# A graph network's recurrent state loaded with two tiles interleaved instead of four, wider lags in the plan, and the TensorE transpose path for two tail groups instead of four

## The chip, the cores and the metric

One NeuronCore of a Trainium2 chip. The metric is the device time of one execution in microseconds (us), medians over several runs. All runs below are in the fast state (single core; granted TensorE clock 0.99 or more as the mean of nearly every run, named where not).

## The reference

`x` is 64 batches of 256 nodes with 128 features, `adj` is 256 x 256. Four layers follow each other, each with a residual and a layer norm. The last is a gated unit of five steps; that is where this change acts:

```python
def step(h, _):
    m_in = jnp.einsum('nm,bmd->bnd', in_matrix, h)     # both matrices are adj here
    m_out = jnp.einsum('nm,bmd->bnd', out_matrix, h)
    av = jnp.concatenate([m_in, m_out], axis=-1)
    u3 = h @ u3_w.T + u3_b
    z = jax.nn.sigmoid(av @ w3_w.T + w3_b + u3)
    r = jax.nn.sigmoid(av @ w4_w.T + w4_b + u3)
    hv = jnp.tanh(av @ w5_w.T + w5_b + (r * h @ u5_w.T + u5_b))
    h = (1.0 - z) * h + z * hv
    return (h, None)
```

## The kernel before

A group is two batches, so four tiles of 128 nodes x 128 features (512 floats in each of 128 partitions); there are 32 groups. Every instruction is entered into a plan with its engine, a cost and a lag (how long after its end another engine may use its result). The plan is made once, while the kernel is built; it fixes each engine's order. The hardware only follows that order and waits where data are not there yet.

```python
class Plan:
    def order(self):
        ...  # each time: of all engines' ready ops take the one that can start first;
                    key = (max(at, t0), op.rank, op.seq)     # then the lower group, then age
        ...
            op.start, op.end = start, start + op.cost + op.lag
            free[op.engine] = start + op.cost
```

The state hT has features in partitions, but the next propagate (`adj @ h`) needs nodes in partitions. Most groups turn it round without TensorE: VectorE transposes 32 x 32 blocks, one DMA writes the result to HBM, one loads it back. The last TAIL groups transpose on TensorE.

```python
def by_node(v):                                   # four tiles interleaved
    return v.ap.rearrange("p (n q) -> p q n", q=Q)

def propagate(self, tag, h, aTs, ins=None, outs=None):
    ps = self.val("bank", "pm" + tag)
    def run():
        o, a = (outs or plain)(ps), (ins or nat)(h)
        for b in range(NB):
            for kt in range(T):
                mm(o[b], a[:, b * T + kt, :], aTs[kt], kt == 0, kt == T - 1)   # h is the stationary operand
    self.pe(pe_cost(N, NB * T), run, [h], [ps])
    return self.copied("m" + tag, ps)

def packed(self, name, src):
    far = self.turned(name, src, "p (k q i) -> p q k i", "p (k j q) -> p q k j")
    t = self.val("w", name)
    def run():
        nc.sync.dma_start(t.ap.rearrange("p (r n) -> p r n", r=4),
                          far.ap.rearrange("(r i) (k n) -> (i k) r n", r=4, k=4))
    self.add("SP", 420, 2350, run, [far], [t])
    return t

# in each of five steps
    if g < G - TAIL:
        if s < STEPS - 1:
            h, ats, ins = self.packed(f"h{s}", hT), a1p, by_node
    else:
        pT = self.transposes(f"h{s}", hT)
        if s < STEPS - 1:
            h = self.copied(f"h{s}", pT)
```

## Time and profile before

| | before |
|---|---|
| time, median of first three runs | 1457.39 us |
| profiled span | 1455.1 us |
| TensorE busy | 97% |
| weight loads of h after DMA / natural | 326 / 190 ns |
| distance of propagate matmuls, h after DMA / natural | 233 / 216 ns |
| TensorE's gaps, 30 us to 185 us before the end | 22.8 us |
| TensorE's gaps in the last 185 us (the drain) | 17.1 us |

A **gap** in this document is worked out from the trace: the distance between the starts of two successive matmuls minus the median distance of matmuls of that kind, where that excess is over 25 ns. It counts all lost time before a matmul, whatever the cause. It is wider than the profile's view of waits, which counts only what exceeds the modelled end of the matmul before. Busy share cannot show it: TensorE reads 97% in both kernels.

### The profile page before, as it was taken

The numbers are of one execution on the slowest core, as the hardware profiler recorded it, in microseconds if no ns is written. First come the engines' busy times: TensorE is split into PE (matmuls) and PEld (weight loads), VectorE is DVE, ScalarE is ACT, GpSimd is POOL, SyncE is SP. The second block draws the span as 40 slices with busy tenths as digits, with TensorE's granted clock in tenths as the row PEclk, the third lists the DMA queues.
The fourth block names the chain that finished last, engine by engine and source line by source line (L and its number), as shares of the span: only waits on it lengthen the run. The fifth ranks groups of instructions, "written<-read, shape, count | busy, mean of one in ns | idle before, by whom it ended". The sixth has DMA issues, their size and how long they took to land.

```text
span 1455.1 us, 16313 instructions
## 1 busy us (share of the span) xinstructions
PE 1407.4 (97%) x5054; PEld 965.1 (66%) x5054; DVE 1008.5 (69%) x2696; ACT 515.7 (35%) x820; POOL 230.7 (16%) x199
## 2 busy tenths in 40 slices
PE   5999999999999999999999999999999999999995
PEld 4866676567666777667676667676677676656652
DVE  3756686758777686676876677776767768757734
ACT  1143423333333333333333333334333333344342
POOL 0411031101210122001211022111111112001200
PEclk9999999999999999999999999999999999999998
DMA  5022232323233223233222333223333322210000
GB/s 165 15 81 79 92 111 87 113 68 109 77 111 109 94 96 107 73 123 95 95 82 90 104 105 96 82 94 95 111 103 96 97 79 88 74 42 30 1 8 15
DMA packets 173830, 123.44 MB, mean 85 GB/s; under 512 B 12592, under 2 KB 148144, under 8 KB 173744
## 3 DMA queue, kind: packets, MB, share of 16 engines
q1 hardware_dynamic: 171440, 121.16, 26.2%
q10 hardware_dynamic: 2304, 1.25, 0.3%
q8 instruction: 40, 0.66, 0.2%
q14 instruction: 46, 0.38, 0.1%
HBM read 61.80 MB, written 60.29 MB: 84 GB/s over the span
## 4 chain that ended last, share of the span: by engine, by line
PE 47%; DVE 5%; DMA 1%; ACT 1%; issue 0%; POOL 0%; SPq 0%; POOLq 0%; DVEq 0%; ACTq 0%
PE pr L191 15%; PE pmg L191 10%; PE ph L191 10%; PE py L191 7%; PE pm L191 3%; PE pmq L191 1%; DVE y L382 1%; DMA h<-dh 1%; DVE d L455 1%; DVE e L455 1%; PE pth L406 1%; DVE st L357 1%; DVE hT L455 1%; ACT hv L449 0%; DVE s L373 0%
## 5 line engine op out<-in xcount | busy, mean ns | idle before, releaser
L368 POOL TENSOR_TENSOR rs<-ve,half 128x4 f32<-128x4 f32 x128 | 141.3, 1106 | 1120.3 <-DVE ve L362 1112.5
L191 PEld LDWEIGHTS pmg<-aTp,h 128*128 128x128 f32 x896 | 220.5, 326 | 39.0 <-DMA h<-dh 12.6
L191 PE MATMUL pmg<-aTp,h 128*128 128x256 f32 x896 | 231.1, 402 | 6.0 <-DMA h<-dh 5.6
L455 DVE TENSOR_TENSOR d<-hv,hT 128x512 f32<-128x512 f32 x160 | 114.3, 715 | 170.6 <-ACT hv L449 170.4
L455 DVE TENSOR_TENSOR rh<-r,hT 128x512 f32<-128x512 f32 x160 | 112.3, 702 | 143.2 <-ACT r L449 143.0
L349 ACT COPY mg<-pmg 128x512 f32<-128x512 f32 x160 | 93.7, 585 | 280.0 <-PE pmg L191 264.8
L382 DVE TENSOR_SCALAR y<-s,mv,rs 128x128 f32<-128x128 f32 x512 | 146.0, 350 | 56.5 <-POOL rs L368 56.0
L191 PE MATMUL pr<-hT,u3T 128*128 128x512 f32 x320 | 163.5, 596 | 3.5 <-DVE hT L455 3.1
L191 PE MATMUL pr<-mg,w4T 128*128 128x512 f32 x320 | 164.4, 595 | 2.3 <-ACT mg L349 2.3
L191 PE MATMUL pr<-mg,w34T 128*128 128x512 f32 x320 | 163.0, 594 | 0.1
L191 PE MATMUL ph<-mg,w5T 128*128 128x512 f32 x320 | 162.8, 592 | 0.0
L191 PE MATMUL ph<-rh,u5T 128*128 128x512 f32 x320 | 162.5, 593 | 0.0
L449 ACT ACTIVATE r<-pr,rb 128x512 f32<-128x512 f32 x160 | 110.0, 687 | 137.5 <-PE pr L191 129.0
L449 ACT ACTIVATE z<-pr,zb 128x512 f32<-128x512 f32 x160 | 109.9, 687 | 133.3 <-PE pr L191 128.4
L449 ACT ACTIVATE hv<-ph,hb 128x512 f32<-128x512 f32 x160 | 109.9, 687 | 48.3 <-PE ph L191 46.4
L414 DVE STREAM_TRANSPOSE th<-hT 128x512 f32<-128x512 f32 x112 | 124.4, 1111 | 1.4
L455 DVE TENSOR_TENSOR e<-z,d 128x512 f32<-128x512 f32 x160 | 115.6, 723 | 3.8
L455 DVE TENSOR_TENSOR hT<-hT,e 128x512 f32<-128x512 f32 x160 | 109.6, 686 | 2.5
L357 DVE BATCH_NORM_STATS2 st<-s 128x6 f32<-128x128 f32 x512 | 109.4, 278 | 1.2
L191 PEld LDWEIGHTS ph<-rh,u5T 128*128 128x128 f32 x320 | 60.4, 190 | 72.6 <-issue 56.9
L191 PEld LDWEIGHTS ph<-mg,w5T 128*128 128x128 f32 x320 | 60.8, 190 | 70.3 <-issue 56.7
L191 PEld LDWEIGHTS pr<-mg,w4T 128*128 128x128 f32 x320 | 59.0, 191 | 51.2 <-issue 43.8
(95 smaller groups left out, 1609.5 us busy)
## 6 DMA issues: line engine op xcount, KB each, us to landing
dh<-th SPq DMA_DIRECT2D x140, 256.0 KB, 2.0
h<-dh SPq DMA_DIRECT2D x112, 256.0 KB, 2.8
x<-in_x_dram SPq DMA_DIRECT2D x32, 256.0 KB, 3.4
out_dram<-y SPq DMA_DIRECT2D x32, 256.0 KB, 2.3
dx<-tx SPq DMA_DIRECT2D x30, 256.0 KB, 2.1
xT<-dx SPq DMA_DIRECT2D x120, 64.0 KB, 2.0
hT<-dh SPq DMA_DIRECT2D x112, 64.0 KB, 2.0
dn<-tn SPq DMA_DIRECT2D x28, 256.0 KB, 2.0
```

What stands on the lines that cost most here:

```text
L191: nc.tensor.matmul(o, lhsT, rhs, start=start, stop=stop, skip_group_check=shared)
L349: self.act(lambda: nc.scalar.copy(t.ap, ps.ap), [ps], [t])
L357: nc.vector.bn_stats(st.ap[:, q * 6:(q + 1) * 6], nat(s)[:, q, :])
L368: lambda: nc.gpsimd.tensor_tensor(rs.ap, ve.ap, half, op=OP.pow), [ve], [rs])
L382: nc.vector.tensor_scalar(nat(y)[:, q, :], nat(s)[:, q, :], mv.ap[:, 2 * q:2 * q + 1], rs.ap[:, q:q + 1], op0=OP.subtract, op1=OP.mult)
L406: nc.tensor.transpose(ps.ap[:, q * P:(q + 1) * P], src.ap[:, q * P:(q + 1) * P], ident)
L414: self.dve(dve_cost(512), lambda: nc.vector.transpose(t.ap.rearrange(outs, k=4, q=Q), src.ap.rearrange(ins, k=4, q=Q)), [src], [t])
L449: self.act(lambda: nc.scalar.activation(t.ap, ps.ap, func, bias=bias, scale=1.0), [ps], [t], act_cost(512) + 100)
L455: self.dve(dve_cost(512), lambda: nc.vector.tensor_tensor(t.ap, a.ap, b.ap, op=op), [a, b], [t])
```

## The change

Intent: make h's weight loads cheap by interleaving only the two tiles of one batch; pay with two DMAs. Let the plan count results and transfers as later than before, so that the fixed order waits less. Keep the TensorE transpose path for two groups.

```diff
-TAIL = 4
+TAIL = 2
@@ Plan.add
+        if engine == "SP":
+            lag += 700
@@
+    def tile_of(v, q):
+        return nat(v)[:, q, :]
+    def pair_of(v, q):
+        return v.ap.rearrange("p (b c t) -> p b t c", b=NB, t=T)[:, q // T, q % T, :]
@@ lags of results: PE, VectorE, ScalarE
-            return self.add("PE", cost, 200, run, reads, writes)
+            return self.add("PE", cost, 260, run, reads, writes)
-            return self.add("DVE", cost, 130, run, reads, writes)
+            return self.add("DVE", cost, 260, run, reads, writes)
-            return self.add("ACT", cost, 70, run, reads, writes)
+            return self.add("ACT", cost, 130, run, reads, writes)
@@ propagate
-                o, a = (outs or plain)(ps), (ins or nat)(h)
+                o, a = (outs or plain)(ps), ins or tile_of
                 ...
-                        mm(o[b], a[:, b * T + kt, :], aTs[kt], kt == 0, kt == T - 1)
+                        mm(o[b], a(h, b * T + kt), aTs[kt], kt == 0, kt == T - 1)
@@ packed
-            far = self.turned(name, src, "p (k q i) -> p q k i", "p (k j q) -> p q k j")
-            t = self.val("w", name)
+            turn, far, t = ...
+            self.dve(dve_cost(512), lambda: nc.vector.transpose(
+                turn.ap.rearrange("p (u j t) -> p u t j", t=T, j=32),
+                src.ap.rearrange("p (u t i) -> p u t i", t=T, i=32)), [src], [turn])
+            self.add("SP", 420, 2000, lambda: nc.sync.dma_start(far.ap, turn.ap), [turn], [far])
             def run():
-                nc.sync.dma_start(t.ap.rearrange("p (r n) -> p r n", r=4),
-                                  far.ap.rearrange("(r i) (k n) -> (i k) r n", r=4, k=4))
-            self.add("SP", 420, 2350, run, [far], [t])
+                for b in range(NB):
+                    nc.sync.dma_start(t.ap.rearrange("p (b r n) -> b p r n", b=NB, r=4)[b],
+                                      far.ap.rearrange("(r i) (k b n) -> b (i k) r n", r=4, b=NB, k=4)[b])
+            self.add("SP", 900, 2300, run, [far], [t])
@@ step
-                        h, ats, ins = self.packed(f"h{s}", hT), a1p, by_node
+                        h, ats, ins = self.packed(f"h{s}", hT), a1p, pair_of
```

More of the change, by code (lines that the diff above doesn't have):

```diff
@@ L431, in packed @@
         def packed(self, name, src):
-            far = self.turned(name, src, "p (k q i) -> p q k i", "p (k j q) -> p q k j")
-            t = self.val("w", name)
+            turn, far, t = self.val("w", "t" + name), self.val("dram", "d" + name), self.val("w", name)
+            self.dve(dve_cost(512), lambda: nc.vector.transpose(
+                turn.ap.rearrange("p (u j t) -> p u t j", t=T, j=32),
+                src.ap.rearrange("p (u t i) -> p u t i", t=T, i=32)), [src], [turn])
+            self.add("SP", 420, 2000, lambda: nc.sync.dma_start(far.ap, turn.ap), [turn], [far])
             def run():
-                nc.sync.dma_start(t.ap.rearrange("p (r n) -> p r n", r=4),
-                                  far.ap.rearrange("(r i) (k n) -> (i k) r n", r=4, k=4))
-            self.add("SP", 420, 2350, run, [far], [t])
+                for b in range(NB):
+                    nc.sync.dma_start(t.ap.rearrange("p (b r n) -> b p r n", b=NB, r=4)[b],
+                                      far.ap.rearrange("(r i) (k b n) -> b (i k) r n", r=4, b=NB, k=4)[b])
+            self.add("SP", 900, 2300, run, [far], [t])
             return t
```

## The prediction

> **What bounds the kernel now.** I read the page first: busy shares, then the 40 slices.
>
> ```profile
> PE 1407.4 (97%) x5054; PEld 965.1 (66%) x5054; DVE 1008.5 (69%) x2696; ACT 515.7 (35%) x820; POOL 230.7 (16%) x199
> PE   5999999999999999999999999999999999999995
> DMA  5022232323233223233222333223333322210000
> ```
>
> TensorE is busy from the second slice to the last but one; nothing else is over 69%. So time changes only where a matmul becomes quicker, where matmuls disappear, or where a gap before a matmul closes. Busy time alone does not say how much a matmul costs, so I next read the timeline of TensorE in mid-kernel. Columns: start, time to the end of the last instruction of the run, instruction, count.
>
> ```profile
> 702.29 2.03 PE L191 MATMUL pmg<-aTp,h 128*128 128x256 f32 x8
> 704.15 0.63 PE L191 MATMUL py<-w0s,xT 128*128 128x256 f32 x2
> ...
> 710.24 1.89 PE L191 MATMUL pm<-aT,y 128*128 128x256 f32 x8
> 711.97 2.03 PE L191 MATMUL pmg<-aTp,h 128*128 128x256 f32 x8
> 713.83 1.02 PE L191 MATMUL pr<-hT,u3T 128*128 128x512 f32 x2
> 714.69 1.05 PE L191 MATMUL py<-w1s,m 128*128 128x128 f32 x8
> ```
>
> Matmuls overlap, so the cost of a run is the distance from its start to the next start. Eight matmuls of 256 columns on natural data (pm) cost 711.97 - 710.24 = 1.73 us, 216 ns each. The same eight on the h that came back by DMA cost 704.15 - 702.29 = 1.86 and 713.83 - 711.97 = 1.86, 233 ns each. Why shows in the groups by form (busy, mean ns; then idle time before):
>
> ```profile
> L191 PEld LDWEIGHTS pmg<-aTp,h 128*128 128x128 f32 x896 | 220.5, 326 | 39.0 <-DMA h<-dh 12.6 <-PE pr L191 5.0 <-issue 4.7
> L191 PEld LDWEIGHTS pmg<-aT,h 128*128 128x128 f32 x128 | 23.8, 190 | 9.2 <-issue 3.6 <-ACT h L349 3.0
> L414 DVE STREAM_TRANSPOSE th<-hT 128x512 f32<-128x512 f32 x112 | 124.4, 1111 | 1.4
> L414 DVE STREAM_TRANSPOSE th<-y 128x512 f32<-128x512 f32 x28 | 19.7, 704 | 0.2
> ```
>
> h is the stationary operand. Where its four tiles are interleaved (one element in 16 bytes) a weight load takes 326 ns, natural 190 ns, and the slower load sets the pace of these short matmuls. The transpose that writes this layout takes 1111 ns against 704 ns for one with contiguous rows.
>
> Last I separated the gaps by time, taking each start-to-start distance minus the median of its kind. From 30 to 1270 us they add up to about 23 us, 13.6 of them before a pmg on a loaded h; from 1270 us to the last matmul about 17. TensorE's first group work starts at 23.8 us and the last matmul at 1446.7, so the head is 23.8 and the end after it 8.4 us. The waits and the transfers that the gaps point to:
>
> ```profile
> PEld pmg L191 <- DMA h<-dh: 12.6, 19, 1.6
> PE pmg L191 <- DMA h<-dh: 5.6, 11, 1.6
> PE pth L406 <- DVE hT L455: 10.1, 6, 3.0
> h<-dh SPq DMA_DIRECT2D x112, 256.0 KB, 2.8
> ```
>
> The third line lies wholly in the drain at the end (the same view over 1270 to 1456 us has the same 10.1). Check of the sum: matmul kinds at their medians 1382.4 (42.37 us for each of 32 groups, 15.2 for the slow weight loads, 10.4 for transposes of the four tail groups, 0.9 for two heads), plus 23.8 + 23 + 17 + 8.4 = 1454.6; the span is 1455.1.
>
> **What the Trainium skill says.** "SBUF — State Buffer", Door 1: The DMA port swizzle: SBUF lines are 16 bytes, and full bandwidth needs at least two hits in a line, so four-byte elements lose it when every access opens a new line. The trace agrees for a step of four elements (326 against 190 ns). With a step of two, which this change makes, each line is hit twice; no instruction here has that step, so this is the main thing I take on trust. "DMA: Bandwidth & Descriptors", Specifications: line rate needs 512 bytes or more per transfer. The new loads move pieces of 64 elements, 256 bytes, half the present size; the trace shows only 512-byte packets for h (most of the packets below 2 KB in the page), and no cost of 256. The same page, Anatomy of one DMA: about 2.0 us are fixed whatever the size; here 64 KB pieces land in 2.0 and 256 KB in 2.0 to 2.8 us, which agrees. "Perfetto Trace Analysis", Identifying the Most-Contended Engine: matmul busy time is a poor measure of distance to the limit; that is why I work with start distances.
>
> **The change part by part.**
>
> *Two tiles interleaved.* The four propagates of each DMA group run at 216 instead of 233 ns: 28 groups x 4 steps x 8 = 896 matmuls x 17 ns = **-15.2 us**, all on TensorE's path. The xT loads keep their step of four (231 ns) and gain nothing. The transpose should fall from 1111 towards 704 ns: 112 x 0.4 = 45 us off VectorE. That is not on the path by itself, but shortens each step's chain by 0.4 us.
>
> *Two DMAs for h.* 240 issues of 128 KB for 112 of 256 KB. One issue now takes 0.37 us on the queue, so the second starts about 0.4 us late and h lands at some 3.2 us (estimate: 2.8 + 0.4) from the first issue. The DMA engines are at 26% for the main queue; 512-byte packets take 16% of all engine time by their durations, h being two fifths of them, so even if 256-byte pieces cost as much each, h adds about 7 points. No bound there: the question is only latency, and a group has ample: a step's chain is about 18 us against 6 groups in flight of 42 us of TensorE work each.
>
> *TAIL 2.* Groups 28 and 29 lose 24 PE transposes each (4 x 6): at 109 ns, 2 x 24 x 0.109 = **-5.2 us** of TensorE. They gain the DMA latency per step. Their propagates then cost the same 216 ns as the natural ones they replace, if the step of two is free. By then groups 30 and 31 have work to fill in, so I count the saving as mostly real; the two last groups, which drain alone, remain on the PE path as now.
>
> *The margin.* No instruction changes, only the plan's order. The plan counts 608 ns for a VectorE operation on 512 elements where the trace has 690, 608 for the transposes of 1111, 1.72 us for a propagate that costs 1.86, and 2.77 us for an h that takes 2.8 plus queueing. So it puts a matmul next that is not yet fed: the 23 us of mid-kernel gaps. With 60 to 130 ns more on each result and 700 on each transfer, it would interpose other work. Planned chain of a group, by its terms: about 88 us in the five steps and some 65 around them; 6 groups of 42 us leave about 250, so the longer lags do not starve TensorE. I expect gaps of 6 to 12 us for 23, say 9: **-14 us**. The drain: 17 us now, 14 to 22 after, because 28 and 29 get slower while 30 and 31 get filled earlier; I take 18: **+1 us**.
>
> *Sum.* 1457.4 - 15.2 - 5.2 - 14 + 1 = **1424 us**. The same from below: floor 1382.4 - 15.2 - 5.2 = 1362.0, plus head 23.8, end 8.4, gaps 9, drain 18 = 1421.2 of span, plus the 2.3 us by which the time exceeds the span now (1457.4 - 1455.1) = 1423.5.
>
> **The rivals.**
>
> *The step of two is not free.* If a weight load then still takes over 216 ns of issue, part of 15.2 stays away. For it: the rate of loading at that step is nowhere in this trace. Against: the skill's statement, and the step of four costs only 17 ns of pace though the load grows by 136, so half of that penalty would be hidden already behind the matmul. It would make 1428 to 1439 us.
>
> *The wait moves into the new loads.* 256-byte pieces and a second issue in the in-order queue land later than the plan's 3.9 us (0.9 + 2.3 + 0.7), and pmg goes on waiting for h. For it: h is already the most frequent wait of TensorE, and the queue blocks on what is planned ahead (VectorE's transposes hold it for 355 us in its own waits). Against: 3.9 is above my 3.2, and the engines are mostly idle. Gaps of about 23 as now would make 1438 us.
>
> *The drain lengthens.* Groups 28 and 29 on the DMA path take some 18 us a step instead of 11 to 14; if 30 and 31 have used up their filler work, each step exposes some us, up to ten in all: 1434 us. Against: each of 30 and 31 carries 42 us of TensorE work, most of it not bound to order.
>
> *The gaps close almost wholly*, middle and drain: 1421 - 6 - 6 = about 1411 us.
>
> **Range and chances.** The two savings by instruction (20.4 us) are alone 1.4%, within 2%. The verdict "faster" needs under about 1428.5 us, so at least 9 us must come from the gaps with the weight loads at full pace. I hold that likelier than not. Slower would need more new waiting than the whole of the savings; nothing in the trace points there. Range 1412 to 1440 us; faster 0.64, within 2% 0.35, slower 0.01.
>
> **What would show it.** Weight loads of pmg on aTp at about 190 ns and eight of them 1.73 us apart: the first step right. Over 200 ns with over 1.75 us: wrong. The transpose th<-hT near 704 ns. 48 fewer PE transposes. h<-dh as 240 issues with TensorE's waits for it under 5 us: the margin right; 15 us or more: the second rival. Gaps before pth still about 10 us and the last matmul about 8 us before the end: the drain unchanged. The prediction is wrong if the time lies above 1440 with the weight loads fast, which would mean that the new order itself idles TensorE.

## The result, and the profile after

1417.3 us (1416.83 to 1421.7, four runs) against 1457.74 us (1457.19 to 1459.53, four runs). The ratio is 0.9727, 95% interval 0.9706 to 0.9748: faster by over 2%. Ratios here are the mean time of one kernel's fast runs over that of the other's of the same rounds, so not quite the ratio of the medians that are quoted.

Busy time by engine of the changed kernel, to set beside the first line in the prediction:

```profile
PE 1376.4 (97%) x5006; PEld 925.0 (65%) x5006; DVE 967.8 (68%) x2706; ACT 511.8 (36%) x812; POOL 224.5 (16%) x199
```

All shares are within a point of before; only the span under them is 40 us shorter. TensorE has 48 matmuls less, the transposes of groups 28 and 29. Its timeline in mid-kernel, same columns as before:

```profile
703.97 1.89 PE L193 MATMUL pm<-aT,y 128*128 128x256 f32 x8
705.70 1.89 PE L193 MATMUL pmg<-aTp,h 128*128 128x256 f32 x8
707.43 1.89 PE L193 MATMUL pmg<-aT,y 128*128 128x256 f32 x8
709.15 1.02 PE L193 MATMUL pr<-hT,u3T 128*128 128x512 f32 x2
```

The loaded h (second line) now costs 707.43 - 705.70 = 1.73 us, the same as natural data in the lines around it; it was 1.86. The groups by form show why:

```profile
L193 PEld LDWEIGHTS pmg<-aTp,h 128*128 128x128 f32 x960 | 187.8, 196 | 42.8 <-issue 19.7 <-PE pr L193 2.9 <-PE ph L193 2.6
L443 DVE STREAM_TRANSPOSE th<-hT 128x512 f32<-128x512 f32 x120 | 84.5, 706 | 1.4
```

A weight load takes 196 ns (326 before) and the transpose 706 ns (1111). The DMA issues:

```profile
h<-dh SPq DMA_DIRECT2D x240, 128.0 KB, 2.5
```

Each half of h lands 2.5 us after its issue, and an issue takes 0.48 us on the queue (0.37 before), so all of h is there some 3.0 us after the first issue (worked out: 0.48 + 2.5).

TensorE's waits in mid-kernel. First the kernel before, 30 to 1270 us (total us, times, longest):

```profile
PE pmg L191 <- DMA h<-dh: 5.6, 11, 1.6
PE pr L191 <- DVE hT L455: 3.1, 5, 1.2
PE pm L191 <- DVE y L382: 0.6, 1, 0.6
PE pr L191 <- DVE mv L361: 0.2, 1, 0.2
```

Then the changed kernel, 30 to 1230 us:

```profile
PE pr L193 <- DVE hT L467: 0.4, 1, 0.4
PE ph L193 <- DVE rh L467: 0.3, 1, 0.3
```

The wait for h is gone altogether, and so are nearly all the others. By the wider count of gaps, mid-kernel fell from 22.8 to 2.7 us.

### The profile page after: what moved, and what is told of

Read it like the earlier page. It is cut to its first block, busy times and chain, and to the rows that moved or that the text cites. A ratio compares the mean times of both kernels' runs of the same rounds, so it can differ in the third digit from the quotient of the medians.

```text
span 1415.3 us, 16464 instructions
## 1 busy us (share of the span) xinstructions
PE 1376.4 (97%) x5006; PEld 925.0 (65%) x5006; DVE 967.8 (68%) x2706; ACT 511.8 (36%) x812; POOL 224.5 (16%) x199
## 3 DMA queue, kind: packets, MB, share of 16 engines
q1 hardware_dynamic: 243056, 127.46, 30.5%
## 4 chain that ended last, share of the span: by engine, by line
PE 95%; DVE 2%; DMA 1%; ACT 1%; issue 0%; POOLq 0%; POOL 0%; SPq 0%; DVEq 0%; ACTq 0%
PE pr L193 29%; PE pmg L193 19%; PE ph L193 19%; PE py L193 16%; PE pm L193 8%; PE pmq L193 4%; DMA x<-in_x_dram 1%; PE pth L414 0%; DVE e L467 0%; DVE d L467 0%; DVE hT L467 0%; PE apow L193 0%; DVE y L390 0%; ACT hv L461 0%; DVE st L365 0%
## 5 line engine op out<-in xcount | busy, mean ns | idle before, releaser
L376 POOL TENSOR_TENSOR rs<-ve,half 128x4 f32<-128x4 f32 x128 | 134.1, 1050 | 1080.9 <-DVE ve L370 1076.2
L193 PE MATMUL pmg<-aTp,h 128*128 128x256 f32 x960 | 225.0, 379 | 0.0
L193 PEld LDWEIGHTS pmg<-aTp,h 128*128 128x128 f32 x960 | 187.8, 196 | 42.8 <-issue 19.7
L467 DVE TENSOR_TENSOR e<-z,d 128x512 f32<-128x512 f32 x160 | 111.7, 702 | 2.2
L193 PEld LDWEIGHTS pr<-mg,w34T 128*128 128x128 f32 x320 | 59.5, 190 | 59.8 <-issue 51.7
```

The lines of the kernel that those rows point to most:

```text
L193: nc.tensor.matmul(o, lhsT, rhs, start=start, stop=stop, skip_group_check=shared)
L376: lambda: nc.gpsimd.tensor_tensor(rs.ap, ve.ap, half, op=OP.pow), [ve], [rs])
L467: self.dve(dve_cost(512), lambda: nc.vector.tensor_tensor(t.ap, a.ap, b.ap, op=op), [a, b], [t])
```

## The experiments

Twelve kernels ran, in three sets of four; each set shared runs of the kernel before (its medians 1457.67, 1457.58 and 1456.62 us). All gave correct results. The table has three terms that make up nearly all of the variation: TensorE's work (all matmuls of the groups at the median distance of their kind), the gaps in mid-kernel, and the gaps in the drain, the last 185 us. Head (up to the first group's first matmul) and end (from the last matmul's start) are 23.0 to 24.8 and 7.8 to 8.9 us in all of them. Work and gaps come from the one profiled execution of each kernel, the time from the median of all its runs. The last column is not measured: it is read from the plan that the kernel makes for itself, namely the gaps in TensorE's planned order in its last 185 us. In mid-kernel the plan of every kernel in the table has no gap, so mid-kernel gaps are what the chip does otherwise than planned.

| kernel | time, us | ratio to before | work | mid gaps | drain gaps | plan's own drain gaps |
|---|---|---|---|---|---|---|
| before | 1457.7 | 1 | 1382 | 22.8 | 17.1 | 14.0 |
| margin alone | 1442.8 | 0.9901 | 1383 | 5.0 | 19.1 | 22.4 |
| two-tile layout alone | 1437.1 | 0.9857 | 1368 | 15.2 | 21.9 | 16.9 |
| the same, h's load planned shorter | 1434.1 | 0.9847 | 1368 | 10.9 | 22.0 | 17.5 |
| TAIL 2 alone | 1458.1 | 1.0004 | 1379 | 19.9 | 23.9 | 17.7 |
| change without margin | 1435.2 | 0.9847 | 1362 | 14.3 | 23.9 | 21.4 |
| change without layout | 1439.8 | 0.9880 | 1379 | 5.5 | 22.1 | 21.4 |
| change with TAIL 4 | 1432.9 | 0.9831 | 1368 | 2.7 | 27.6 | 25.8 |
| margin on transfers only | 1438.5 | 0.9872 | 1362 | 6.3 | 33.2 | 29.1 |
| margin on results only | 1420.7 | 0.9752 | 1362 | 3.1 | 21.1 | 21.3 |
| **the change** | 1417.3 | 0.9727 | 1362 | 2.7 | 18.3 | 19.3 |
| change, last group ranked first | 1410.2 | 0.9684 | 1362 | 2.7 | 10.5 | 11.4 |
| change, xT in two tiles too | 1418.4 | 0.9747 | 1359 | 2.2 | 30.2 | 25.1 |
| both of these | 1405.4 | 0.9644 | 1359 | 2.2 | 10.0 | 12.1 |

My theory (A): the layout saves work, and the margin closes the mid-kernel gaps. Its rival (B): the layout closes the gaps as well, because it shortens each step's chain; the margin does little.

**One part at a time.** The margin alone:

```diff
 # kernel before, plus:
+        if engine == "SP":
+            lag += 700
 # and the lags 260, 260, 130 for 200, 130, 70
```

> The kernel before with the longer lags in the plan and nothing else (four interleaved tiles, TAIL 4). Theory A (the plan's margin closes the gaps of TensorE): gaps between 30 and 1270 us fall from 22.8 to some 3 to 6 us, weight loads stay at 326 ns; time 1437 to 1441 us. Theory B (the gaps closed because the new layout shortens each step's chain, through the transpose of 0.7 instead of 1.1 us and no slow propagates): the gaps stay above 15 us; time 1450 to 1458 us.

Measured: 1442.8 us, mid gaps 5.0. The mechanism of A held, the time came 2 us above its band, since the drain grew by 2. Weight loads are untouched (325 ns). TensorE's mid-kernel waits in this run, 30 to 1254 us, show that an order alone did it, with the old transfers:

```profile
PE ph L193 <- DVE rh L457: 0.8, 1, 0.8
PE pmg L193 <- DMA h<-dh: 0.2, 1, 0.2
```

The layout alone:

```diff
 # changed kernel, but
-            lag += 700
+            lag += 0
 # lags 200, 130, 70 as before; TAIL = 4
```

> The kernel before with two interleaved tiles loaded by two DMAs and nothing else (no margin, TAIL 4). Weight loads 196 ns, propagate matmuls 216 ns apart: minus 15.2 us. Theory A: mid-kernel gaps stay at 15 to 25 us, before pmg on h; time 1438 to 1446 us. Theory B: gaps fall to under 8 us; time 1424 to 1432 us.

Measured: 1437.1 us, between the two bands; work down by 14.8 us as worked out. But mid gaps fell to 15.2, and of those only 1.6 stand before a propagate on h (13.6 in the kernel before). The waits, 30 to 1250 us:

```profile
PE pr L193 <- DVE hT L467: 4.6, 8, 1.5
PE ph L193 <- DVE rh L467: 1.7, 3, 0.8
PE pmg L193 <- DMA h<-dh: 0.5, 1, 0.5
```

So B is right for one kind of gap, the one that the prediction gave to the margin alone: the late h. Either part is enough to close it. The other kind, matmuls on fresh results of VectorE (hT, rh), the layout does not close: gaps before the matmuls that read hT or rh were 6.4 us in the kernel before and are 11.9 here. Longer lags on results do close it: 1.9 us are left with the margin alone, 1.3 in the change.

TAIL 2 alone:

```diff
-TAIL = 4
+TAIL = 2
```

> The kernel before with TAIL 2 and nothing else. 48 fewer PE transposes save 5.2 us, but 8 propagates of groups 28 and 29 then load strided weights (64 matmuls x 17 ns, 1.1 us more). Both theories: 1450 to 1457 us; above 1457 us would mean that the drain takes back what the transposes save.

Measured: 1458.1 us, 14 runs, a microsecond above the range, which was the sign set for a drain that takes the saving back. The work fell by about 4 us, mid gaps by 3; the drain grew by 7 and took it all back.

**One part left out.** Without the margin:

```diff
 # changed kernel, lags 200, 130, 70 and no 700 on transfers
```

> The changed kernel without the margin (two interleaved tiles, two DMAs, TAIL 2). Theory A: the gaps come back, 15 to 23 us between 30 and 1270 us; time 1430 to 1440 us. Theory B: within 5 us of the changed kernel, 1417 to 1422 us.

Measured: 1435.2 us, A's band. Of the 17.9 us that the margin is worth here, 11.6 are mid gaps (14.3 against 2.7) and 5.6 drain. In mid-kernel (30 to 1247 us) it waits for results, not for transfers:

```profile
PE pr L193 <- DVE hT L467: 4.7, 8, 1.5
PE ph L193 <- DVE rh L467: 1.7, 3, 0.8
```

Without the layout:

```diff
 # kernel before with the margin and TAIL = 2
```

> The changed kernel with the old layout (four interleaved tiles, one DMA), so margin and TAIL 2 only. Theory A (parts add up): propagate matmuls of 960 again 233 instead of 216 ns apart, plus 16.3 us on 1417.3, gaps still small: 1432 to 1436 us. Theory B (the layout also closes the gaps): gaps of 10 us or more come back as well, 1443 us or more.

Measured: 1439.8 us. Between A's and B's figures: 16.8 us more work (16.3 expected), mid gaps 5.5 as A says, but a drain longer by 3.8.

With TAIL 4:

```diff
-TAIL = 2
+TAIL = 4
```

> The changed kernel with TAIL 4. 48 more PE transposes add 5.2 us of TensorE work. If the drain is unaffected by which path groups 28 and 29 take: 1421 to 1424 us. If the PE path still shortens the drain: within 2 us of 1417.3 us.

Measured: 1432.9 us, far off both expectations. Work is 5 us more, as counted, and mid gaps are identical; the drain is 27.6 instead of 18.3 us. TAIL 2 is worth nothing in the kernel before and 15.6 us in this one. A part whose worth depends so much on its company does not act through its own cost. That raised the question of what sets the drain.

**Which half of the margin.**

```diff
 # changed kernel with one half of the margin only
-            lag += 700        # results only
-    260, 260, 130             # transfers only: 200, 130, 70
```

> The changed kernel with the margin on transfers alone (700 ns), the old lags on results. If the gaps were late DMA loads: mid-kernel gaps under 5 us, 1417 to 1422 us. If they were late results of VectorE and ScalarE: gaps of 10 us or more, 1427 us or more.

> The changed kernel with the margin on results alone, the old lags on transfers. If the gaps were late DMA loads: gaps of some 10 us before pmg on h, 1426 us or more. If they were late results: 1417 to 1422 us.

Measured: transfers only 1438.5 us, results only 1420.7 us. The second is what late results would give; the first has mid gaps of 6.3 us, between the two theories' figures. By time alone the transfers' half would look harmful (1435.2 without any margin). By the table it is not: it halves the mid gaps (14.3 to 6.3), and a drain of 33.2 us hides that. The results' half leaves 3.1 us of mid gaps, so with the new layout it is the half that matters; 700 ns more on transfers then takes off another 0.4 us of mid gaps and brings another draw of the drain.

The traces also show how long a result really takes. In the 12 cases in the kernel before where TensorE waited for VectorE's hT, its matmul started 747 to 840 ns after the hT instruction did (median 838). The old plan counted 738 ns (608 + 130), so it was too short every time; the new one counts 868. Whether measured costs in the plan would do as well as a margin was not tested.

**Why the layout closed the late h.** In its own planned cost the new load carries 0.43 us more (900 + 2300 against 420 + 2350 ns), which could be a margin in disguise (theory C), against a really shorter chain (D).

```diff
 # layout alone, but
-            self.add("SP", 900, 2300, run, [far], [t])
+            self.add("SP", 900, 1870, run, [far], [t])
```

> The run with the two-tile layout alone (no margin, TAIL 4), but the plan counts the two loads of h with 2.77 us from first issue to landing, as in the kernel before, not 3.20 us. In the layout-only run the gaps before pmg on h fell from 13.6 to 1.6 us without any margin. Theory C (the 0.43 us that the new load's planned cost adds is a hidden margin): gaps before pmg return to 6 us or more. Theory D (the real chain is shorter, transpose 0.7 instead of 1.1 us, and the propagate keeps the plan's pace): gaps before pmg stay under 3 us. The time should be 1435 to 1439 us under D, 1440 us or more under C.

Measured: gaps before the propagate 2.3 us (1.6 with the longer lag), so C falls, and D is left; 1434.1 us, below D's band by a microsecond. Which of D's two halves does it, the transpose shorter by 0.4 us or the propagate that now keeps the plan's 1.72 us, was not separated.

**What sets the drain.** At their ends the last two columns of the table go together: where the plan itself leaves 11 to 12 us without work for TensorE, the chip loses 10, where it leaves 25 to 29, the chip loses 28 to 33. Between them they do not: TAIL 2 alone has 17.7 planned and 23.9 lost, the margin alone 22.4 and 19.1. Theory E: the drain is made by the plan, whose greedy rule lets the lower group go first, so that the last group is left alone. Theory F: latencies that the plan does not hold make it. The test changes nothing but the rank of the last group's recurrent steps:

```diff
-            op = plan.add(engine, cost, lag, self.g, run, reads, writes, after)
+            self.count += 1
+            rank = 28.5 if self.g == G - 1 and self.count >= 35 else self.g
+            op = plan.add(engine, cost, lag, rank, run, reads, writes, after)
```

> The changed kernel, but the recurrent steps of the last group are ranked ahead of groups 29 and 30 in the plan; nothing else. Theory E (the drain's gaps are the plan's own, and its order alone sets them): the plan's own gaps in the last 185 us fall from 19.3 to 11.4 us, so the measured ones from 18.3 to some 10 to 12 us and the time from 1417.3 to 1408 to 1412 us. Theory F (the drain is set by latencies that the plan does not hold): 1415 us or more.

Measured: 1410.2 us, drain gaps 10.5, inside E's band. TensorE's timeline shows what is different. In the changed kernel the last steps belong to one group alone (brackets: idle before, and releaser):

```profile
1383.50 0.66 PE L414 MATMUL pth<-ident,hT 128*128 128x128 f32 x4 [2.96 <-DVE hT L467]
...
1384.86 1.97 PE L193 MATMUL pmg<-aT,h 128*128 128x256 f32 x8
...
1394.50 0.63 PE L414 MATMUL pth<-ident,hT 128*128 128x128 f32 x4 [3.11 <-DVE hT L467]
...
1396.32 3.08 PE L193 MATMUL pmg<-aT,h 128*128 128x256 f32 x8
...
1407.02 0.63 PE L414 MATMUL pth<-ident,hT 128*128 128x128 f32 x4 [3.05 <-DVE hT L467]
```

Each such step takes 11 us or more (the last 12.5, part of it at a granted clock of 0.72) and leaves TensorE idle for 3 of them, while VectorE finishes the new state. With the last group ranked first, two groups end nearly together and fill each other's waits until the last step:

```profile
1394.20 0.66 PE L417 MATMUL pth<-ident,hT 128*128 128x128 f32 x4 [0.76 <-DVE hT L470]
1398.69 1.08 PE L417 MATMUL pth<-ident,hT 128*128 128x128 f32 x4 [3.83 <-DVE mv L372]
```

The rank and the point from which it holds were chosen among 18 variants by the planned end alone (the other 17 are not on record); the chip then ran one.

So the order alone moves the drain, as E says, but F is not empty. The six kernels with the old lags on results lose 2.5 to 6.2 us more in the drain than their plans leave. Those with longer lags on results stay within 3.3 us of theirs, save the one with xT in two tiles (below), which lost 5.1 more, at a lower clock.

The clock is the other thing that the plan does not hold. The traces show TensorE's granted clock at 0.5 for stretches of 3.4 or 6.8 us in most drains; in the changed kernel this is 1395.3 to 1398.7 us, and the eight matmuls at 1396.32 take 3.08 us, where those at 1384.86 take 1.97. Of the drain gaps, those at matmuls that start in such a stretch make 0 us in the kernel before, 1.6 in the change, 0.3 with the last group ranked first, and 5.4 with TAIL 4. So 3.8 of the 9.3 us by which the drain with TAIL 4 is longer stand there, and 1.3 of the 7.8 us that the rank saves. Whether an order with long waits itself brings the lower clock was not tested.

**The same layout for xT.** The input's weight loads still step over four elements. With xT in two tiles, its features in permuted order and the rows of w0 permuted alike:

```diff
+    w0p = const.tile([P, 2, C], F32, name="w0p")
+    for k in range(4):
+        nc.scalar.dma_start(w0p.rearrange("(j r) t n -> r j t n", r=4)[k], w0s[32 * k:32 * (k + 1), 0:2])
...
-                xT = self.brought("xT", self.turned("x", x_, ...))
+                xT = self.packed_x("x", x_)      # like packed: one write, two loads
...
-                        mm(o, ... by_node(xT)[:, b * T + t, :], w0s[:, 0:2, :], ...)
+                        mm(o, pair_of(xT, b * T + t), w0p, ...)
```

> The changed kernel with the same two-tile layout for xT as well (weights w0 in a permuted order, two loads instead of four). The weight loads py on xT fall from 309 to 196 ns and their matmuls from 231 to 216 ns apart: minus 3.6 to 4 us of TensorE. The plan's own drain grows from 19.3 to 25.1 us, plus 5.8. Theory E: 1417 to 1421 us, the saving eaten by the drain. If the drain did not follow the plan: 1412 to 1415 us.

Measured: 1418.4 us. The weight loads are what was expected. In the changed kernel, then here (240 of the 256):

```profile
L193 PEld LDWEIGHTS py<-w0s,xT 128*128 128x128 f32 x256 | 69.4, 309 | 8.6 <-issue 2.2 <-PE pr L193 0.7 <-PE py L193 0.7
```

```profile
L193 PEld LDWEIGHTS py<-w0p,xT 128*128 128x128 f32 x240 | 46.1, 196 | 15.1 <-issue 8.7 <-PE py L193 1.2 <-PE pr L193 0.5
```

The work fell by 3.6 us and no time was gained: the drain of another order took it back, as E said. (The profiled execution of this kernel was its slowest, 1424.7 us at a granted clock of 0.988; 10.8 of its 30.2 us of drain gaps stand where the clock is at 0.5. The median run is 6 us shorter, so its drain was probably about 24 us; it was not traced.)

Both together, with the last group ranked ahead of group 30 from its second layer on:

```diff
 # xT in two tiles, and
+            rank = 29.5 if self.g == G - 1 and self.count >= 20 else self.g
```

> xT in two tiles, and the last group from its layer 1 on ranked ahead of group 30 (not 29). The plan's own drain is 12.1 us. Theory E: minus 3.8 us for xT, minus 7 us for the drain: 1404 to 1410 us, the fastest of all. Theory F: 1412 us or more.

Measured: 1405.4 us (1403.49 to 1405.62), ratio 0.9644 to the kernel before: the fastest kernel here, by 12 us against the change (medians of different sets).

## Why the prediction was right or wrong

The time was 1417.3 us for 1424 predicted, inside the range, and "faster" was the likelier class. By its steps:

- **Weight loads at a step of two: right.** 196 ns, matmuls 216 ns apart. The layout alone saves 14.8 us of work for 15.2 worked out. Of the first rival nothing is left.
- **The transpose: right** (706 ns for 704). I said that it is not on the path by itself. As part of the layout it may be one of the reasons why h was no longer late; this is not separated.
- **Two DMAs: right that they stay off the path.** h lands about 3.0 us after the first issue (3.2 estimated). The DMA share rose by 4.3 points, 26.2% to 30.5% on the main queue, not by 7: a packet of 256 bytes took 18 ns in the trace, one of 512 bytes 27. The second rival did not appear.
- **TAIL 2: right in work, wrong in the role I gave it.** The transposes' 5.2 us are saved. But alone it gained nothing, and within this change it is worth 15.6 us, 9.3 of them through the drain.
- **The margin: the mis-sized term.** "I expect gaps of 6 to 12 us for 23, say 9: -14 us." Measured 2.7, so -20.1 us. The plan's figures were too short, as the prediction said (738 ns for a result of VectorE that took up to 840). This term, 6.3 us, is nearly the whole distance between 1424 and 1417.3. I also named the wrong owner for part of it: the late h, 13.6 of the 22.8 us, is closed by the layout alone too.
- **The drain: right size, weak reason.** I took 18 us; it was 18.3. The prediction argued from DMA latency of groups 28 and 29. The runs show 10.0 to 33.2 us for plans that differ in small ways, with the plan's own order as the cause in the two runs that changed the rank alone, and a part lost at a halved clock. That 18 came out is the draw of this order, not a confirmation of the argument. The third rival, a longer drain, is what seven of the nine runs with parts of the change did (21.9 to 33.2 us).
- **Two readings were a little off** and change nothing: VectorE's operations on 512 elements took 686 to 723 ns in the kernel before (means by kind), not 690, and a group's planned chain with the longer lags, redone from the plan, is 147.5 us, not 88 + 65.

The result is thus 20 us of work (layout and transposes), 20 us of mid-kernel gaps (margin, for the late h also the layout), and about 1 us given back in the drain.

What stays open: how much of the mid-kernel gaps comes from each engine's lag, which half of the shorter chain rescues h, whether measured costs would do as well as a margin, what halves the clock in the drain, and whether the drain's last 10 us can go.

## What to carry to other kernels

When an order is planned ahead, count a result as later than it is measured (here 868 ns for 747 to 840), as long as enough independent work is in flight: the order then interposes work that is ready, and here that was worth as much as the cheaper weight loads. When judging a small change to such a plan, split the time into work, gaps in the middle and gaps in the drain before judging it; a drain that moves by 10 us for any reason makes good parts look useless and useless ones good. Interleave a stationary fp32 operand by two tiles and not by four (196 against 326 ns a load here), and look at the distance between matmuls, not at their busy time, to see what it is worth.

## What the Trainium skill lacked or had wrong

- "SBUF — State Buffer", Door 1: The DMA port swizzle: the rule of two hits per 16-byte line held, for weight loads and for VectorE's transposes, which the page does not name. Weight loads: 190 ns contiguous, 196 ns at a step of two fp32, 326 ns at four. Transposes of 512 elements: 704, 706 and 1111 ns.
- "Perfetto Trace Analysis", Identifying the Most-Contended Engine: the page gives the weight loads' busy share, beside the share of peak arithmetic, as a good measure of distance to the limit. Here it went from 66% to 65% while the kernel became 2.7% faster; a load of 326 ns cost only 17 ns of pace. The distance between matmul starts was the measure that worked.
- "DMA: Bandwidth & Descriptors", Specifications: it gives 512 bytes as the least for line rate. The page works out an overhead for descriptors of 256 bytes under "Why small descriptors are slow (HBM only)", but has no measured time for one on such loads. Measured (medians): 18 ns against 27 ns a packet, so 14.2 against 19.0 bytes per ns on an engine, and no wait of TensorE for it.
- No page: what a statically planned order loses when its lags are short, and how widely its drain scatters (10.0 to 33.2 us of TensorE's gaps in fourteen orders of nearly the same work).
